# A graph-attention layer: the scaling of gathered rows takes its factors through a DVE operation that reads the newest logit

## Chip, cores, metric

One core of one Trainium2 chip. The metric is the device time of the whole program in microseconds (us). Every run below was in the fast state. Engines: PE is TensorE's matrix multiply and PEld its weight load, DVE is VectorE, ACT ScalarE, POOL GpSimd, SP SyncE.

## The reference, cut to what matters

4096 nodes with 512 features, 8 heads of 64, float32. A row of `adj` has some 17 ones; attention runs over these alone.

```python
hs = layer_norm(h_source); ht = layer_norm(h_target)
q = (ht @ Wq + bq) / sqrt(64); k = hs @ Wk + bk; v = hs @ Wv + bv
logits = where(adj != 0, q @ k^T per head, -1e30)
ctx = softmax(logits) @ v
ht = ht + ctx @ Wo + bo                  # h_target is normalized here, too
ht = layer_norm(ht)
out = layer_norm(x + ht + gelu(ht @ W1) @ W2)
```

## The kernel before

Phases that overlap: projecting all K/V rows to DRAM (`kvd`), turning the adjacency rows into lists of neighbours, and attention with the feed-forward layer. The 4096 targets are sorted by degree and handled in 32 tiles of 128. A tile is worked in supergroups of up to S neighbours (211 supergroups in all): for each, POOL gathers K/V rows, DVE multiplies K by q and reduces to logits `lg`, ACT takes the exponential, DVE multiplies V by it, and PE sums over neighbours by transposing into one PSUM tile, `cps`.

Before a tile's attention its `front` makes q. It is a generator, advanced one step (`yield`) at a time by the supergroups of earlier tiles. The first part below is where the change acts. A scheduler orders the instructions of each engine and may draw one forward past others when it expects its inputs to be there, so the position of a `yield` does not fix the place in an engine's queue. A data dependence does.

```python
def front(i, idle=0):
    rec = recs[i]                                  # the tile's record: targets, neighbours, mean and rstd
    tq = sp.tile([P, 2 * D], F32, name="tq", bufs=3)
    t = tq[:, :D]
    gather(t, h_target, rec[:, TGT:TGT + 1])       # POOL: indirect DMA of 128 rows
    for _ in range(1 + idle):
        yield
    m = rec[:, RST:RST + 2].bitcast(F32)
    nc.scalar.activation(t, t, AF.Identity, bias=m[:, 1:2], scale=m[:, 0:1])    # ACT, line 990
    yield
    pt = ps.tile([P, KC, P], F32, name="t", bufs=2)
    for kc in range(KC):
        nc.tensor.transpose(pt[:, kc, :], t[:, kc * P:(kc + 1) * P], ident)     # PE, line 994
    hT = tq[:, D:].rearrange("p (c t) -> p c t", c=KC)
    for kc in range(KC):
        nc.scalar.activation(hT[:, kc, :], pt[:, kc, :], AF.Identity, ...)      # ACT, line 997
    yield
    yield
    # ... q projection: matmuls with wq on PE, line 1003, three yields
    nc.vector.scalar_tensor_tensor(tq[:, :D], pq, HD ** -0.5, bqr, ...)         # DVE, line 1008
    tqs[i] = tq

def prefetch(i):
    # ...
    rec = sp.tile([P, E0 + MAXE], I32, name="rec", bufs=7)
    nc.gpsimd.dma_start(rec[:, :RW], recs_d[part][r0:r0 + P, :])                # record load
    recs[i] = rec

# attention, one supergroup k of tile i
nc.vector.tensor_tensor(kv[:, :n, :D], kv[:, :n, :D], tq..., ALU.mult)          # DVE, line 1209
lg = sp.tile([P, S, H], F32, name="lg")
nc.vector.tensor_reduce(lg[:, :n, :], kv..., AX.X, ALU.add)                     # DVE, line 1213
if j0 > 0:
    nc.scalar.activation(p[:, j0:j0 + n, :], lg[:, :n, :], AF.Exp)              # ACT, line 1217
advance()                                          # steps of fronts and of finished tiles' tails
# ...  the value products (line 1173) and transposes into cps (line 1181) of the supergroup before
```

Of the kernel before, what the change touches and what calls it, by code (L numbers as in the profile page):

```python
# [12 lines left out]
ALU = mybir.AluOpType  # L13
# [430 lines left out]
def adj_resnorm_kernel(  # L444
# [33 lines left out]
    nc = tc.nc  # L478
# [51 lines left out]
    def rows(a, g):  # L530
        return a[g * GR:(g + 1) * GR, :].rearrange("(j p) d -> p j d", p=P)

    with tc.tile_pool(name="keep", bufs=1) as keep:
# [17 lines left out]
        with ExitStack() as late:  # L551
# [26 lines left out]
            def xrows(n):  # L578
                return ring[:, 12 + n % 5, :].rearrange("p (j d) -> p j d", j=G)
# [183 lines left out]
            def keep_rest():  # L763

                while held:
                    nc.sync.dma_start(*held.pop())
# [97 lines left out]
            def project(order, t=None):  # L864


                state, scales = {}, {}

                def request(n, t=None):
                    if n >= len(order):  # L870
                        return
                    if t is None:
                        t = xrows(n)
                        nc.sync.dma_start(t, rows(x, order[n]))
                    state[n] = t

                def measure(n):
                    if n >= len(order):
                        return
                    mv = ip.tile([P, G, 2], F32, name="mv")  # L880
                    for j in range(G):
                        stats(ip, state[n][:, j, :], mv[:, j, :], "n1")
                    scales[n] = rstd_of(ip, mv, G, "n1")

                def scale(n):
                    if n >= len(order):
                        return
                    t, (rs, nm) = state[n], scales.pop(n)
                    for j in range(G):
                        nc.scalar.activation(t[:, j, :], t[:, j, :], AF.Identity,  # L890
                                             bias=nm[:, j:j + 1], scale=rs[:, j:j + 1])

                def turn(n):
                    if n >= len(order):
                        return
                    t = state[n]
                    hT = sp.tile([P, KC, GR], F32, name="h2T")
                    for k2 in range(KC // 2):
                        pt = (psi if k2 else ps).tile([P, 2, GR], F32, name="pt" if k2 else "t",
                                                      bufs=1 if k2 else 2)  # L900
                        for k in range(2):
                            kc = k2 * 2 + k
                            for j in range(G):
                                nc.tensor.transpose(pt[:, k, j * P:(j + 1) * P],
                                                    t[:, j, kc * P:(kc + 1) * P], ident)
                        for k in range(2):
                            kc = k2 * 2 + k
                            if n == 0:

                                nc.vector.tensor_scalar(hT[:, kc, :], pt[:, k, :],  # L910
                                                        s1c[:, kc:kc + 1], b1c[:, kc:kc + 1],
                                                        op0=ALU.mult, op1=ALU.add)
                            else:
                                nc.scalar.activation(hT[:, kc, :], pt[:, k, :], AF.Identity,
                                                     bias=b1c[:, kc:kc + 1],
                                                     scale=s1c[:, kc:kc + 1])
                    state[n] = t, hT

                def source(n, j):
                    g, hT = order[n], state[n][1]  # L920
                    if asked or moms:
                        kvr = sp.tile([P, 2 * D], F32, name="tq", bufs=3)
                    else:

                        kvr = ring[:, 8 + (n * G + j) % 3, :]
                    for half, w in enumerate((wk, wv)):
                        pkv = psi.tile([P, D], F32, name="pq", bufs=3)
                        for kc in range(KC):
                            nc.tensor.matmul(pkv, hT[:, kc, j * P:(j + 1) * P], w[:, kc, :],  # L929
                                             start=kc == 0, stop=kc == KC - 1)  # L930
                        nc.scalar.copy(kvr[:, half * D:(half + 1) * D], pkv)  # L931
                    r0 = 1 + (g * G + j) * P
                    nc.scalar.dma_start(kvd[r0:r0 + P, :], kvr)
                    return 7.8

                with tc.manual_schedule(engines={mybir.EngineType.DVE}):
                    request(0, t)
                    measure(0)
                    scale(0)
                    turn(0)  # L940
                    request(1)
                    measure(1)
                    scale(1)
                for n in range(2, 4):
                    request(n)
                measure(2)
                yield 0.0
                for n in range(len(order)):
                    for j in range(G):
                        cost = source(n, j)  # L950
                        if j == 0:
                            request(n + 4)
                            measure(n + 3)
                            turn(n + 1)
                        else:
                            scale(n + 2)
                            del state[n]
                        yield cost


            recs, tqs, h2Ts, done, ready = {}, {}, {}, set(), []

            def gather(dst, table, idx):
                nc.gpsimd.indirect_dma_start(  # L964
# [15 lines left out]
            def front(i, idle=0):  # L980


                rec = recs[i]
                tq = sp.tile([P, 2 * D], F32, name="tq", bufs=3)
                t = tq[:, :D]
                gather(t, h_target, rec[:, TGT:TGT + 1])
                for _ in range(1 + idle):
                    yield
                m = rec[:, RST:RST + 2].bitcast(F32)
                nc.scalar.activation(t, t, AF.Identity, bias=m[:, 1:2], scale=m[:, 0:1])  # L990
                yield
                pt = ps.tile([P, KC, P], F32, name="t", bufs=2)
                for kc in range(KC):
                    nc.tensor.transpose(pt[:, kc, :], t[:, kc * P:(kc + 1) * P], ident)
                hT = tq[:, D:].rearrange("p (c t) -> p c t", c=KC)
                for kc in range(KC):
                    nc.scalar.activation(hT[:, kc, :], pt[:, kc, :], AF.Identity,  # L997
                                         bias=b1r[:, kc:kc + 1], scale=s1c[:, kc:kc + 1])
                yield
                yield  # L1000
                pq = ps.tile([P, D], F32, name="t", bufs=2)
                for kc in range(KC):
                    nc.tensor.matmul(pq, hT[:, kc, :], wq[:, kc, :], start=kc == 0,  # L1003
                                     stop=kc == KC - 1)
# [3 lines that stand above are left out]
                nc.vector.scalar_tensor_tensor(tq[:, :D], pq, HD ** -0.5, bqr,  # L1008
                                               op0=ALU.mult, op1=ALU.add)
                tqs[i] = tq  # L1010
# [5 lines left out]
            kvs, rests, fronts = {}, {}, {}  # L1016
# [10 lines left out]
            def step(gens, i):  # L1027

                if i in gens and next(gens[i], StopIteration) is StopIteration:
                    del gens[i]  # L1030
# [115 lines left out]
            def first_fronts():  # L1146

                for i in range(EARLY):
                    prefetch(i)
                for i in range(EARLY):  # L1150
                    fronts[i] = front(i)
                while fronts:
                    go_on()
                    yield 4.0

            def attention():
# [41 lines left out]
                for group in GROUPS:  # L1198
# [3 lines left out]
                    for i in group:  # L1202
                        cps = ps.tile([P, KC, P], F32, name="cps", bufs=2)
                        while k < len(SG) and SG[k][0] == i:
                            _, j0, n = SG[k]
                            while i not in tqs:
# [3 lines left out]
                                                    tq[:, :D].unsqueeze(1).to_broadcast([P, n, D]),  # L1210
                                                    ALU.mult)
                            lg = sp.tile([P, S, H], F32, name="lg")
                            nc.vector.tensor_reduce(lg[:, :n, :],  # L1213
                                                    kv[:, :n, :D].rearrange("p j (h d) -> p j h d", h=H),
                                                    AX.X, ALU.add)
# [218 lines left out]
            def other_lists():  # L1434
                for cost in ed:
                    yield 1.5 * cost
                yield from sort(1)

            _weave((att, 0), (chain(feed(g) for g in range(len(GROUPS))), 0), (other_lists(), WAIT),
# [36 lines left out]
```

## Time and profile before

| | before |
|---|---|
| time, median of 3 (range) | 1851.66 us (1851.42 to 1855.57) |
| profiled span | 1847.4 us |
| PE busy | 1693.9 us, 92% |
| DVE busy | 1428.8 us, 77% |
| ACT busy | 1222.2 us, 66% |
| POOL busy | 971.7 us, 53% |

The prediction shows the busy rows and the waits of the line that the change touches. From the list of waits, these five lines matter for the rivals (who waited, for what: us in total, times, longest):

```profile
POOL kv L964 <- PE cps L1181: 157.2, 79, 17.0
...
DVE kv L1209 <- DMA kv<-kvd,rec: 71.2, 27, 11.7
ACT p L1217 <- DVE lg L1213: 69.3, 37, 9.3
ACT gt L1319 <- PE pf L1316: 66.7, 17, 8.0
...
DVE tq L1008 <- PE t L1003: 42.6, 10, 9.8
```

POOL waits for PE to free K/V slots; DVE waits for K/V rows, and for PE's projection of q before it can evict it; ACT waits for logits and for the feed-forward matmuls. A long row does no harm in itself: it tells who was idle, not whether the end moved.

One hole in PE's row as the timeline shows it (start, busy us, engine, line, operation, shapes; in brackets the wait in us and what ended it):

```profile
1294.69 3.62 PE L1316 MATMUL pf<-h2T,w 128*128 128x256 f32 x16
...
1302.12 3.70 PE L1003 MATMUL t<-wq,tq 128*128 128x512 f32 x8 [3.81 <-ACT tq L997]
```

PE finished what stood ahead, and then stood 3.81 us for ACT's eviction at line 997, which follows a blocked scaling in ACT's queue. Holes of this sort are what the change is after.

### The profile page before, as it was taken

The numbers are of one execution on the slowest core, as the hardware profiler recorded it, in microseconds if no ns is written. First come the engines' busy times: TensorE is split into PE (matmuls) and PEld (weight loads), VectorE is DVE, ScalarE is ACT, GpSimd is POOL, SyncE is SP. The second block draws the span as 40 slices with busy tenths as digits, with TensorE's granted clock in tenths as the row PEclk, the third lists the DMA queues.
The fourth block names the chain that finished last, engine by engine and source line by source line (L and its number), as shares of the span: only waits on it lengthen the run. The fifth ranks groups of instructions, "written<-read, shape, count | busy, mean of one in ns | idle before, by whom it ended". The sixth has DMA issues, their size and how long they took to land. (4 is left out here: it accounts for less than half of the span.)

```text
span 1847.4 us, 22879 instructions
## 1 busy us (share of the span) xinstructions
PE 1693.9 (92%) x7030; PEld 1101.0 (60%) x7030; DVE 1428.8 (77%) x2596; ACT 1222.2 (66%) x3121; POOL 971.7 (53%) x834
## 2 busy tenths in 40 slices
PE   7999884697988989999998998999999999999997
PEld 3444332475655656767676656666666666666664
DVE  6999855999989838686968989979787797988200
ACT  5777634587877646686767867687767676787311
POOL 1000153856546577656567787776574665664001
PEclk9999987898999989999999999999999999999999
DMA  9999949988876738677769878687676767775000
GB/s 350 374 388 374 348 156 350 348 300 303 285 271 209 243 96 313 230 252 260 275 225 315 293 265 295 221 298 253 233 265 216 251 225 247 236 248 170 12 12 25
DMA packets 144396, 463.27 MB, mean 251 GB/s; under 512 B 20628, under 2 KB 25800, under 8 KB 144264
## 3 DMA queue, kind: packets, MB, share of 16 engines
q0 software_dynamic: 96656, 342.64, 54.2%
q1 hardware_dynamic: 39792, 96.00, 14.5%
q10 hardware_dynamic: 7816, 23.08, 3.3%
q8 instruction: 58, 0.95, 0.2%
q14 instruction: 74, 0.61, 0.1%
HBM read 430.76 MB, written 30.89 MB: 250 GB/s over the span
## 5 line engine op out<-in xcount | busy, mean ns | idle before, releaser
L964 POOL DMA_INDIRECT kv<-kvd,rec x603 | 744.9, 1235 | 395.1 <-PE cps L1181 157.2
L1325 PE MATMUL po<-w,gt 128*128 128x512 f32 x1024 | 470.4, 603 | 9.7 <-ACT gt L1319 7.2
L1316 PE MATMUL pf<-h2T,w 128*128 128x256 f32 (+1 forms) x2176 | 466.6, 368 | 1.1 <-issue 0.7
L1316 PEld LDWEIGHTS pf<-h2T,w 128*128 128x128 f32 x2176 | 388.7, 191 | 66.6 <-issue 22.4
L1209 DVE TENSOR_TENSOR kv<-kv,tq 128x1536 f32<-128x1536 f32 (+2 forms) x211 | 352.0, 1676 | 82.4 <-DMA kv<-kvd,rec 71.2
L1193 ACT ACTIVATE kv<-kv,pa 128x64 f32<-128x64 f32 x1520 | 390.8, 336 | 4.1
L1213 DVE TENSOR_REDUCE lg<-kv 128x24 f32<-128x1536 f32 (+2 forms) x211 | 350.2, 1667 | 1.1 <-DVE kv L1209 0.2
L1325 PEld LDWEIGHTS po<-w,gt 128*128 128x128 f32 x1024 | 190.7, 194 | 210.3 <-issue 201.5
L1181 PE MATMUL cps<-ident,kv 128*128 128x128 f32 x2008 | 264.6, 280 | 51.1 <-DMA kv<-kvd,rec 24.2
L1181 PEld LDWEIGHTS cps<-ident,kv 128*128 128x128 f32 x2008 | 238.2, 145 | 120.2 <-DVE kv L1173 51.5
L1173 DVE TENSOR_TENSOR kv<-kv,p 128x1024 f32<-128x1024 f32 (+1 forms) x211 | 251.5, 1194 | 41.2 <-ACT p L1217 28.8
L687 POOL TENSOR_TENSOR n_rs<-n_ve,mhalf 128x2 f32<-128x2 f32 (+2 forms) x51 | 47.7, 936 | 340.8 <-DVE n_ve L680 139.8
L728 ACT ACTIVATE kv<-kv 128x1024 uint8<-128x1024 int32 x128 | 134.7, 1054 | 76.8 <-DMA kv<-in_adj_dram 40.6
L1319 ACT ACT_TABLE_LOAD x104 | 133.4, 1283 | 1.6
L735 DVE MAX8 cand<-kv 128x8 uint16<-128x103 uint16 (+1 forms) x640 | 130.2, 252 | 1.7 <-issue 0.7
L1003 PE MATMUL t<-wq,tq 128*128 128x512 f32 x256 | 119.9, 611 | 12.1 <-ACT tq L997 12.1
L1319 ACT ACTIVATE gt<-pf 128x512 f32<-128x512 f32 x128 | 76.4, 597 | 81.0 <-PE pf L1316 66.7
L929 PE MATMUL pq<-wk,h2T 128*128 128x512 f32 x256 | 121.6, 618 | 5.2 <-ACT tq L931 3.7
L929 PE MATMUL pq<-wv,h2T 128*128 128x512 f32 x256 | 118.5, 606 | 6.7 <-ACT kv L931 5.5
L1107 PE MATMUL t<-wo,rb 128*128 128x512 f32 x256 | 120.7, 614 | 0.0
L990 ACT ACTIVATE tq<-tq,rec 128x512 f32<-128x512 f32 x32 | 26.0, 813 | 142.8 <-DMA tq<-in_L_gnn_h_target_dram,rec 136.3
L1217 ACT ACTIVATE p<-lg 128x24 f32<-128x24 f32 (+2 forms) x179 | 38.9, 218 | 94.6 <-DVE lg L1213 69.3
(156 smaller groups left out, 1603.3 us busy)
## 6 DMA issues: line engine op xcount, KB each, us to landing
kv<-in_adj_dram SPq DMA_DIRECT2D x128, 512.0 KB
kvd<-tq ACTq DMA_DIRECT2D x24, 512.0 KB
kv<-kvd,rec POOLq DMA_INDIRECT x603
kv<-in_L_gnn_h_target_dram SPq DMA_DIRECT2D x32, 256.0 KB
kv<-in_x_dram SPq DMA_DIRECT2D x15, 512.0 KB
rest_d<-gid SPq DMA_DIRECT2D x32, 160.0 KB
w<-in_L_gnn_W_dram SPq DMA_DIRECT2D x4, 1024.0 KB
kvd<-kv ACTq DMA_DIRECT2D x8, 512.0 KB
```

The costliest lines, as they stand in the source:

```text
L728: nc.scalar.activation(sg, a, AF.Sign, accum_out=dpart[:, i, h:h + 1])
L735: nc.vector.max(cand[:, h * SQ + s, :], wd[:, w0:w1])
L929: nc.tensor.matmul(pkv, hT[:, kc, j * P:(j + 1) * P], w[:, kc, :], start=kc == 0, stop=kc == KC - 1)
L964: nc.gpsimd.indirect_dma_start(out=dst, out_offset=None, in_=table[:, :], in_offset=bass.IndirectOffsetOnAxis(ap=idx, axis=0))
L1173: nc.vector.tensor_tensor(v4, v4, p[:, j0:j0 + m, :].unsqueeze(3) .to_broadcast([P, m, H, HD]), ALU.mult)
L1181: nc.tensor.matmul(cps[:, c, :], kv[:, j, D + c * P:D + (c + 1) * P], ident, is_transpose=True, start=j0 + j == 0 and c == 0, stop=j0 + n ...
L1193: nc.scalar.mul(v, v, pa[:, hd:hd + 1])
L1209: nc.vector.tensor_tensor(kv[:, :n, :D], kv[:, :n, :D], tq[:, :D].unsqueeze(1).to_broadcast([P, n, D]), ALU.mult)
L1213: nc.vector.tensor_reduce(lg[:, :n, :], kv[:, :n, :D].rearrange("p j (h d) -> p j h d", h=H), AX.X, ALU.add)
L1316: nc.tensor.matmul(pf[:, k, :], w1[(f0 + k) // KC][:, kc, (f0 + k) % KC * P:((f0 + k) % KC + 1) * P], h2T[:, kc, :w], start=kc == 0, stop= ...
L1319: nc.scalar.activation(gt, pf, AF.Gelu_apprx_tanh)
L1325: nc.tensor.matmul(po[j], gt[:, k, j * P:(j + 1) * P], w2[(f0 + k) // KC][:, (f0 + k) % KC, :], start=False, stop=f0 + k == FC - 1, skip_g ...
```

## The change

Its intent: in the schedule before, the scaling of a tile's row is placed so early that ACT reaches it while the row gather is still under way. ACT then stands, and what is queued behind stands with it (at 1299.68 us it started the scaling after 4.25 us of waiting, and only then, at 1300.40, the copy behind it). The change makes the scaling depend on something that comes later by itself: a DVE operation that writes the two factors `m` back unchanged (`max(m, m)`; the bypassed operand is the newest logit). It also stores the last list's spare candidates at the end of the list phase, and makes the first two tiles, which have no logits yet, use a late K/V projection.

```diff
@@ source(): K/V projection @@
                         nc.scalar.copy(kvr[:, half * D:(half + 1) * D], pkv)
+                    if n >= 14:
+                        latest[:] = [kvr[:, 0:1]]
@@ front() @@
                 m = rec[:, RST:RST + 2].bitcast(F32)
+                nc.vector.scalar_tensor_tensor(m, m, latest[-1], m, op0=ALU.bypass, op1=ALU.max)
                 nc.scalar.activation(t, t, AF.Identity, bias=m[:, 1:2], scale=m[:, 0:1])
@@ first_fronts() @@
                     fronts[i] = front(i)
+                    step(fronts, i)
+                while not latest:
+                    yield None
@@ attention() @@
                             lg = sp.tile([P, S, H], F32, name="lg")
+                            latest[:] = [lg[:, 0, 0:1]]
@@ other_lists() @@
                     yield 1.5 * cost
+                keep_rest()
                 yield from sort(1)
```

(The list `latest` is also created; blank lines are cut.) From here on "the tie" is the added DVE operation. The lines of the changed kernel stand some lines lower: 990 is 995 there, 994 is 999, 997 is 1002, 1003 is 1008, 1008 is 1013, 1173 is 1181, 1181 is 1189, 1209 is 1217, 1213 is 1222, 1217 is 1226, 1138 is 1143, 1316 is 1325, 1319 is 1328. The tie itself is line 994 there.

More of the change, by code (lines that the diff above doesn't have):

```diff
@@ L958, in project @@
                         yield cost
-            recs, tqs, h2Ts, done, ready = {}, {}, {}, set(), []
+            recs, tqs, h2Ts, done, ready, latest = {}, {}, {}, set(), [], []
             def gather(dst, table, idx):
```

## The prediction

> **What bounds the kernel now.** I read the page first (busy shares and slices), then the table of groups by line, then the waits, then one line's own view, then the busy time in stretches of 50 us, and last the timelines around the longest stalls.
>
> ```profile
> PE 1693.9 (92%) x7030; PEld 1101.0 (60%) x7030; DVE 1428.8 (77%) x2596; ACT 1222.2 (66%) x3121; POOL 971.7 (53%) x834
> PE   7999884697988989999998998999999999999997
> DVE  6999855999989838686968989979787797988200
> ACT  5777634587877646686767867687767676787311
> ```
>
> TensorE is the fullest engine, and in the last slices it is the only one with work: attention ends near 1700 us and TensorE then works alone for 137 us on the feed-forward layer. Its work is fixed, so the span is that work plus the holes in TensorE's row. Busy shares hide some holes, so I also measured the spacing of matmul starts against the usual spacing of each form (109 ns for a 128x128 transpose, 215 for 256 columns, 429 for 512). That gives 1634 us of work and 193 us of excess spacing; the rest of the span is its two ends. Of the excess some 62 us lie before 300 us (projections and the switch to attention), 67 us between 300 and 600 us, and 64 us after. The stretches show how unevenly it lies:
>
> ```profile
> 300.00:350.00 50.00, 20.50 (x104) 16.10 (x104) 39.06 (x45) 22.53 (x82) 39.42 (x33) 0.66 1.00 386
> ...
> 700.00:750.00 50.00, 50.00 (x237) 35.32 (x236) 44.50 (x45) 38.91 (x116) 34.73 (x31) 1.00 0.84 289
> ...
> 1100.00:1150.00 50.00, 45.16 (x206) 31.35 (x204) 44.20 (x44) 35.14 (x97) 39.72 (x31) 1.00 0.91 318
> ```
>
> (Columns: window, length, then busy us and count of PE, PEld, DVE, ACT, POOL, then clock, DMA share, GB/s.) From 700 us on TensorE is nearly full; no other engine is.
>
> The instruction that the change touches is the scaling of the gathered h rows on ScalarE, line 990:
>
> ```profile
> L990 ACT ACTIVATE tq<-tq,rec 128x512 f32<-128x512 f32 x32 | 26.0, 813 | 142.8 <-DMA tq<-in_L_gnn_h_target_dram,rec 136.3 <-issue 6.5
> ...
> ACT tq L990 <- DMA tq<-in_L_gnn_h_target_dram,rec: 136.3, 28, 14.0
> ...
> PEld t L994: 7.9, 2
> PE t L994: 7.2, 2
> ```
>
> It works 26.0 us and holds ScalarE idle for 142.8 us, 28 waits of up to 14.0 us for the row gather to land. The last two lines are from the line's own view, "who waited for it": its direct consumer on TensorE lost only 7.2 us, in two places. So the 143 us harm only through whatever stands behind the blocked instruction in ScalarE's queue.
>
> **What the Trainium skill says.** (1) "Trainium Kernel Development and Optimization", Performance Expectations, warns that matmul busy time is a bad measure because matmuls are pipelined. The trace agrees: the 92% row holds 1634 us of work in 1847 (88%). (2) "Perfetto Trace Analysis", Per-instruction lifecycle (DVE / Act), puts the semaphore wait before the reported start. Agrees: the 813 ns contain no wait, the 142.8 us stand as idle time before it. (3) "DMA: Bandwidth & Descriptors", Anatomy of one DMA, fits 2.0 us plus bytes/436e3 per DMA, an estimate of 2.6 us for these 256 KB. The trace is slower: in the cases where ScalarE was already waiting, issue to use took about 3.4 to 7.7 us (590.0 to 593.6, 513.3 to 521.0). (4) "VectorE: DVE Perf Modes", the errata on SBUF sources, charges a fixed cost per instruction. Agrees: a scalar_tensor_tensor on 128x2 takes 163 ns here (line 692), though it handles two columns.
>
> **The change, part by part.** First, 32 added DVE instructions, `m = max(m, m)` on 128x2, which read the newest logit (for the first two tiles, the newest projection) without using it. Cost: 32 x 163 ns = 5.2 us of DVE, on an engine that is 77% busy; I charge 1 us to the path. Second, what moves. The order of instructions shows that the scheduler, which had drawn line 990 forward, must now place it behind that logit. Counting softmax exponentials ahead of it on ScalarE, it stands later in 27 of 32 tiles, by 1 to 9 supergroups (mostly 2 to 5); tiles 0, 1, 3, 8 and 20 do not move. TensorE's order of the transposes and projections that follow is practically the same against the context matmuls, and so is DVE's `tq` evacuation, and POOL's gathers but for two. This is then a change of ScalarE's queue alone. In the attention part a supergroup takes about 6.6 us (1395 us over 211), so two to five are 13 to 33 us, more than nearly all of the waits. What remains are tiles 0, 8 and 20, with 6.5, 5.9 and 6.9 us, and remnants where the move is one place: I expect ScalarE's wait at this line to fall from 143 to about 20 us.
>
> What is that worth? I followed each wait forward along ScalarE's queue: everything behind it could come earlier by the wait, less every later idle gap of ScalarE, which would absorb it. Wherever a TensorE stall ended by such a ScalarE instruction, I took the smaller of the stall and the surviving shift: 1.4 and 7.1 us (525 to 534), 0.9 (436), 2.0 (897), 3.6 (1089), 1.8 (1151), 1.7 (1244), 3.8 (1302), 2.0 (1388), 1.4 (1664): sum 25.7 us. The longest of them I checked in the timeline:
>
> ```profile
> 521.00 0.81 ACT L990 ACTIVATE tq<-tq,rec 128x512 f32<-128x512 f32 x1 [6.72 <-DMA tq<-in_L_gnn_h_target_dram,rec]
> ...
> 523.83 0.60 ACT L1319 ACTIVATE gt<-pf 128x512 f32<-128x512 f32 x1
> ...
> 533.06 1.92 ACT L1138 ACTIVATE h2T<-t,cols 128x256 f32<-128x256 f32 x4
> ...
> 534.12 1.11 PE L1090 MATMUL t<-ident,rb 128*128 128x128 f32 x4 [7.10 <-ACT h2T L1138]
> ```
>
> Between the block and the late eviction stands a gelu whose matmuls ended only at 522.4, so the eviction could come some 1.4 us earlier, not 6.7. That takes 5.7 us off: 20 us direct. The same walk finds up to 59 us of DVE waits that would shrink; DVE is not the bound, so I choose 5 us of them to come through to TensorE as less waiting for the value products (line 1173). Sum: 20 + 5 - 1 = 24 us.
>
> Third, new waits. The DVE instruction needs the tile's record in SBUF, which only the gathers needed before, and DVE's queue blocks behind it. For tiles 8 and 20 the record load was issued at most 5.4 and 6.6 us before the gather, beside logits that follow closely; I charge 2 us together. Fourth, the store of the last candidates (`keep_rest`): the last store was already issued at 603.5 us, the first gather that reads it at 863 us, and the queue's order is unchanged. Worth 0. The start-up line in the first two tiles: ScalarE's block at 266 to 273 us turns into a block on DVE's instruction behind a list step that ended at 274.4; the last store of K/V comes after sign activations that wait for adjacency loads in both versions. Worth 0 to 1 us; I take 0.
>
> Total 22 us: 1851.7 - 22 = **1830 us**.
>
> **Rivals.**
> A: the wait was hidden anyway. For it: the direct consumer lost 7.2 us; TensorE is in order and its order doesn't change; between 300 and 600 us its stalls are mostly start-up, where DVE has the work. Around 953 us the longest sort of block (10.1 us) lies beside a DVE gap of 9.4 us that comes from late K/V gathers, and would stay. Against it: seven stalls are ended by line 997 or 1193 or an eviction directly behind a block. It would give 1840 to 1852.
> B: the gain multiplies. Attention is a ring: ScalarE's exponential, DVE's product, TensorE's transposes, freed slots, POOL's gathers (157.2 us idle for TensorE's line 1181), then DVE again. If ScalarE's blocks pace that ring, most of the 115 us of excess after 300 us could go, and I would see 1790 to 1812. Against it: TensorE has no excess between 700 and 800 us (0.1 us), with a block of 14.0 us at 760 in it.
> C: a wait takes the removed one's place. Scaling now comes two to three supergroups before the evacuated `tq` is needed on DVE (before: mostly four to eight), and the chain of transposes, four evictions and eight passes of 0.43 us each or more must fit. DVE already waited 42.6 us for that `tq`, 9.8 us at most. Lateness there, or DVE standing for a record or scatter, would give 1845 to 1870. Against it: TensorE's order put the transposes mostly 15 to 40 us after the old scaling, usually more than the move.
>
> **Range and chances.** The middle is the mechanism at its counted size. Between A and a mild B lies 1812 to 1850, which I hold 8 times in 10. Two per cent is 37 us, below 1814.6: it needs B, 0.13. Slower than 1888.7 would need C everywhere, 0.02. Within 2%: 0.85.
>
> **What would show it.** Right: ScalarE's idle time before the scaling 10 to 30 us; TensorE's work by spacing the same and its excess after 300 us near 93 instead of 115 us; stalls at 1089, 1244, 1302 and 1388 gone; DVE's 32 new instructions near 0.16 us each with under 10 us idle before them. Wrong: the idle time gone and the excess unchanged (A), the K/V gathers' wait for TensorE's transposes down by half (B), or DVE's wait before `tq` well above 43 us (C).

## The result, and the profile after

A ratio here is the mean time of one kernel's fast runs over that of the other's in the same rounds, so it is not quite the ratio of the medians quoted beside it. Intervals are 95%.

| | before | after |
|---|---|---|
| time, median | 1853.62 us (4 runs) | 1828.03 us (4 runs: 1816.57 to 1828.37) |
| ratio | | 0.9847 (0.9806 to 0.9888), "same" by the 2% rule |
| profiled span | 1847.4 | 1826.4 |
| granted clock | 0.964 | 0.963 |
| PE work by spacing of matmul starts | 1633.9 | 1633.5 |
| PE excess spacing | 193.3 | 173.4 |

By the ratio that is 28 us (0.0153 of 1853.62), by the medians 25.6, by the two profiled executions 21.0. PE's work did not change and its excess fell by 19.9 us, so the gain of the profiled pair lies nearly all in PE's holes. The page's row:

```profile
PE 1687.8 (92%) x7030; PEld 1102.5 (60%) x7030; DVE 1432.2 (78%) x2628; ACT 1222.0 (67%) x3119; POOL 973.8 (53%) x834
ACT  5767634487987637676767777778777676787311
```

The shares hardly differ: a gain of 1.5% can't be read from them. DVE has 32 instructions more and 3.4 us more work. The own view of the scaling says what happened (first row: count, shortest/median/longest ns, first and last start; then what ended ACT's idle time before it, and below the cut who waited for it):

```profile
L995 ACT ACTIVATE tq<-tq,rec x32: 798/806/852, 278.1 to 1633.4; 128x512 f32<-128x512 f32 x32
...
  DMA tq<-in_L_gnn_h_target_dram,rec: 15.3, 2
  DVE rec L994: 13.5, 4
  issue: 2.1, 2
...
  PE t L999: 15.4, 5
```

142.8 us of idle time became 30.9. Two waits for a gather are left (tile 8 with 6.3 us and tile 20 with 9.0), and four for the tie, of which 11.3 us is the first tile's. PE's transposes now lose 15.4 us here, 7.2 before; 7.4 us of it is the first tile's. The tie's own view:

```profile
L994 DVE SCALAR_TENSOR_TENSOR rec<-rec,lg x30: 171/215/267, 341.3 to 1631.4; 128x2 f32<-128x2 f32 x30
...
  DMA rec<-rec: 4.7, 2
```

Its median is 215 ns. The 32 durations sum to 6.9 us, of which DVE's busy row shows 3.4. DVE stood 4.7 us in two places for a record that had not landed. Of the waits:

```profile
POOL kv L966 <- PE cps L1189: 161.4, 89, 8.7
ACT p L1226 <- DVE lg L1222: 114.1, 52, 11.0
ACT gt L1328 <- PE pf L1325: 87.8, 20, 9.6
DVE kv L1217 <- DMA kv<-kvd,rec: 82.9, 22, 12.3
...
DVE tq L1013 <- PE t L1008: 46.5, 14, 8.3
```

Part of ACT's freed time turns up as other waits. The rows of ACT waiting for logits and for feed-forward matmuls grew by 44.8 and 21.1 us, 66 of the 112 us that went from the scaling's row. Such rows are no measure of the gain: the start-only kernel below, which kept the gather waits and gained nothing, has 100.1 and 72.2 us in them. ACT's busy time is the same (1222.2 and 1222.0).

The same three stretches of 50 us as in the prediction:

```profile
300.00:350.00 50.00, 20.01 (x80) 15.93 (x81) 37.64 (x41) 22.47 (x79) 38.86 (x32) 0.56 0.99 385
...
700.00:750.00 50.00, 50.00 (x227) 34.14 (x226) 37.38 (x47) 39.62 (x106) 32.55 (x29) 1.00 0.82 282
...
1100.00:1150.00 50.00, 45.88 (x209) 33.04 (x210) 49.27 (x51) 40.90 (x110) 41.43 (x29) 0.97 0.83 293
```

The first two gained nothing. In the third PE has a little more work done, and DVE 5 us more. Summed over stretches of 100 us, PE's excess spacing fell most from 500 to 600 us (20.4 to 9.8), from 1200 to 1300 (8.0 to 1.8), from 400 to 500 (18.5 to 14.1), from 1300 to 1400 (4.1 to 0.1) and from 1100 to 1200 (10.3 to 6.7), and rose from 300 to 400 (28.0 to 31.9), from 1000 to 1100 (9.5 to 12.8) and from 800 to 900 (3.9 to 6.6). The stretches are of each kernel's own time, so a stall that moved over an edge counts as a fall and a rise.

The two timelines, first the stall at 534 us that the prediction showed:

```profile
526.70 0.60 ACT L1328 ACTIVATE gt<-pf 128x512 f32<-128x512 f32 x1
527.19 1.92 ACT L1143 ACTIVATE h2T<-t,cols 128x256 f32<-128x256 f32 x4
...
529.45 0.85 ACT L995 ACTIVATE tq<-tq,rec 128x512 f32<-128x512 f32 x1
...
528.26 0.66 PE L1095 MATMUL t<-ident,rb 128*128 128x128 f32 x4 [2.74 <-ACT h2T L1143]
```

Before, ACT did the scaling at 521.0, with 6.72 us of waiting, then two gelus, at 523.83 and 532.33, and 0.73 us after the start of the second the eviction of `h2T` at 533.06. Now the two gelus are at 514.70 and 526.70, the eviction is 0.49 us behind the second, and the scaling comes after both, without a wait. PE's stall went from 7.10 to 2.74 us.

The other place is the hole at 1302 us. PE's order is the same there, and the matmul that waited (the 4790th of PE's 7030) now starts at 1287:

```profile
1283.79 3.62 PE L1325 MATMUL pf<-h2T,w 128*128 128x256 f32 x16
1287.25 3.60 PE L1008 MATMUL t<-wq,tq 128*128 128x512 f32 x8
```

PE runs from one group into the next without a hole.

### The profile page after: what moved, and what is told of

It is laid out like the page before. It is cut to its first block, busy times and chain, and to the rows that moved or that the text cites. A ratio compares the mean times of both kernels' runs of the same rounds, so it can differ in the third digit from the quotient of the medians.

```text
span 1826.4 us, 22937 instructions
## 1 busy us (share of the span) xinstructions
PE 1687.8 (92%) x7030; PEld 1102.5 (60%) x7030; DVE 1432.2 (78%) x2628; ACT 1222.0 (67%) x3119; POOL 973.8 (53%) x834
## 5 line engine op out<-in xcount | busy, mean ns | idle before, releaser
L966 POOL DMA_INDIRECT kv<-kvd,rec x603 | 751.4, 1246 | 376.2 <-PE cps L1189 161.4
L1334 PE MATMUL po<-w,gt 128*128 128x512 f32 x1024 | 464.9, 597 | 6.2 <-ACT gt L1328 6.0
L1217 DVE TENSOR_TENSOR kv<-kv,tq 128x1536 f32<-128x1536 f32 (+2 forms) x211 | 351.7, 1675 | 88.1 <-DMA kv<-kvd,rec 82.9
L1189 PE MATMUL cps<-ident,kv 128*128 128x128 f32 x2008 | 269.0, 283 | 53.4 <-issue 23.5
L1189 PEld LDWEIGHTS cps<-ident,kv 128*128 128x128 f32 x2008 | 243.3, 147 | 122.4 <-issue 68.9
L1181 DVE TENSOR_TENSOR kv<-kv,p 128x1024 f32<-128x1024 f32 (+1 forms) x211 | 250.9, 1193 | 23.8 <-ACT p L1226 20.3
L1328 ACT ACTIVATE gt<-pf 128x512 f32<-128x512 f32 x128 | 76.3, 597 | 99.2 <-PE pf L1325 87.8
L1226 ACT ACTIVATE p<-lg 128x24 f32<-128x24 f32 (+2 forms) x179 | 39.2, 219 | 128.8 <-DVE lg L1222 114.1
L1112 PE MATMUL t<-wo,rb 128*128 128x512 f32 x256 | 116.5, 597 | 0.0
L929 PEld LDWEIGHTS pq<-wk,h2T 128*128 128x128 f32 x256 | 50.3, 203 | 72.9 <-issue 59.1
```

The lines of the kernel that those rows point to most:

```text
L929: nc.tensor.matmul(pkv, hT[:, kc, j * P:(j + 1) * P], w[:, kc, :], start=kc == 0, stop=kc == KC - 1)
L966: nc.gpsimd.indirect_dma_start(out=dst, out_offset=None, in_=table[:, :], in_offset=bass.IndirectOffsetOnAxis(ap=idx, axis=0))
L1181: nc.vector.tensor_tensor(v4, v4, p[:, j0:j0 + m, :].unsqueeze(3) .to_broadcast([P, m, H, HD]), ALU.mult)
L1189: nc.tensor.matmul(cps[:, c, :], kv[:, j, D + c * P:D + (c + 1) * P], ident, is_transpose=True, start=j0 + j == 0 and c == 0, stop=j0 + n ...
L1217: nc.vector.tensor_tensor(kv[:, :n, :D], kv[:, :n, :D], tq[:, :D].unsqueeze(1).to_broadcast([P, n, D]), ALU.mult)
L1328: nc.scalar.activation(gt, pf, AF.Gelu_apprx_tanh)
```

## The experiments

Theory: ACT's queue, blocked by the gather in front of ready work, delayed evictions that PE needed; the tie moves the scaling behind them. Rivals for the source of the gain: the start-up lines or the store of the candidates; a nonlinear effect on the ring of K/V slots; the later place of the tile's transposes on PE rather than the wait. Rivals for what limits it: DVE's added work, or DVE's waits for q and for records. The edits below are against the changed kernel unless they say otherwise. The kernel before ran on the same chip in each call (medians 1856.79, 1854.42, 1854.88 and 1857.33 us in the four calls).

A kernel that has only the added store was built but not run: its order of instructions on all five engines is that of the kernel before (the author's comparison; no trace of it is kept).

### The tie without the store

```diff
 def other_lists():
-                keep_rest()
```

> The change without its second part (the earlier store of the last candidates). The order of instructions on every engine is the same as in the changed kernel, so my theory expects 1828 us, within 3 us. A rival that gives the store a share of the 25 us would expect 1835 us or more.

Measured: 1825.65 us (6 runs, 1818.73 to 1838.51), ratio 0.9831 (0.9797 to 0.9866). Its order of instructions on every engine is that of the changed kernel. The whole gain is here, so the store is worth nothing that can be seen.

### The tie in the first half, and in the second half

```diff
+                if i < 16:            # the other kernel: if i >= 16
                     nc.vector.scalar_tensor_tensor(m, m, latest[-1], m, ...)
```

> Only tiles 0 to 15 take their factors through the DVE operation; the other 16 scalings stand on ScalarE where they stood before. By spacing of matmul starts the changed kernel lost 10 us less than the kernel before up to 900 us and 12 us less after. My theory (each freed wait pays where it stands) expects 1843 us, 1838 to 1847. A rival that puts the gain into the start of attention or into one place expects nearly all of it here (1830) or nothing (1852).

> The other half: only tiles 16 to 31 are tied. My theory expects 1841 us, 1836 to 1846, and the gains of both halves to add up to that of the whole, within 5 us. The rival of one early place expects 1852 us.

Measured: 1844.61 us, ratio 0.9939 (0.9906 to 0.9972), and 1841.41 us, ratio 0.9923 (0.9886 to 0.9961). The waits of the scaling that are left, first with the tie up to tile 15, then with the tie from 16:

```profile
ACT tq L996 <- DMA tq<-in_L_gnn_h_target_dram,rec: 82.7, 16, 9.9
```

```profile
ACT tq L996 <- DMA tq<-in_L_gnn_h_target_dram,rec: 64.4, 12, 13.9
```

Each half loses the waits of its own tiles and keeps the others'. The gains, 0.61 and 0.77%, sum to 1.38% (25.6 us of 1856.79), beside 1.69% for the whole in the same call; the intervals of the halves are about 0.35% wide to each side, so the sum and the whole agree. That fits a sum of local gains, spread over the whole attention part. It is no sign of a ring that speeds up only when all waits are gone.

### The wait put back, everything else kept

A copy of one column onto itself, on ACT, ahead of the tie: it needs the gathered row and nothing else, so the scheduler may place it as early as it did the scaling before.

```diff
+                nc.scalar.copy(t[:, 0:1], t[:, 0:1])
                 nc.vector.scalar_tensor_tensor(m, m, latest[-1], m, ...)
                 nc.scalar.activation(t, t, AF.Identity, bias=m[:, 1:2], scale=m[:, 0:1])
```

> The changed kernel with one 128x1 copy of a gathered column onto itself on ScalarE, which the scheduler puts where the scaling stood before (the same place among the exponentials in 31 of 32 tiles). It brings back ScalarE's wait for the row gather and nothing else; the scaling stays late. My theory (it is the blocked queue that costs) expects ScalarE to idle 110 to 150 us before these copies and the time to return to 1846 to 1858 us. The rival (the order of the scaling itself, or the later transposes, makes the gain; the waits were hidden) expects 1828 to 1835 us.

Measured: 1847.93 us (1842.54 to 1854.79), ratio 0.9965 (0.9929 to 1.0001). In the order of ACT's queue the copy stands where the scaling stood before in 31 of 32 tiles. With the copies left out, the order of instructions on DVE and POOL is that of the changed kernel throughout, and on PE and ACT but for five neighbours that changed places; the real scaling has the same number of exponentials ahead of it in all 32 tiles. So this kernel is the changed kernel plus the old wait. The copy's own view, and one row of the waits (from line 994 on, this kernel's lines stand one lower again than the changed kernel's):

```profile
L994 ACT COPY tq<-tq x32: 191/191/194, 275.7 to 1645.0; 128x1 f32<-128x1 f32 x32
...
  DMA tq<-in_L_gnn_h_target_dram,rec: 136.4, 27
...
ACT p L1227 <- DVE lg L1223: 76.9, 43, 9.3
```

The stall at 534 us again, in this kernel:

```profile
523.84 0.19 ACT L994 COPY tq<-tq 128x1 f32<-128x1 f32 x1 [8.56 <-DMA tq<-in_L_gnn_h_target_dram,rec]
...
534.38 0.60 ACT L1329 ACTIVATE gt<-pf 128x512 f32<-128x512 f32 x1
534.87 1.93 ACT L1144 ACTIVATE h2T<-t,cols 128x256 f32<-128x256 f32 x4
...
535.94 1.11 PE L1096 MATMUL t<-ident,rb 128*128 128x128 f32 x4 [6.70 <-ACT h2T L1144]
```

ACT's order around it is the changed kernel's, and the stall is back: 7.10 us before, 2.74 in the changed kernel, 6.70 here. So is the hole at 1302 us (3.81, none, 3.23).

The wait is back (136.3 us before, 136.4 here), ACT's wait for logits fell back from 114.1 to 76.9 (before: 69.3) and that for feed-forward matmuls from 87.8 to 62.7 (before: 66.7), and PE's excess is 194.0 (before 193.3, after 173.4). Of the 31.4 us that the tie gave in this call (0.0169 of 1856.79), 24.9 are gone and 6.5 are left (0.0035), with an interval that touches no gain. The tie and the later places of the real scaling are all still there. So the removed wait on ACT is the cause of at least most of the gain. The remaining 6.5 us, if real, may come from the 0.8 us of the scaling itself, which no longer stands right behind each wait (the copy takes 0.19); that was not tested. The start-up lines are not the source (the start alone, below, gives 1.0009).

### The scaling one supergroup later still

```diff
-                for _ in range(1 + idle):
+                for _ in range(1 + idle + 2 * (i >= EARLY)):
```

> The changed kernel with every scaling from tile 2 on one supergroup (about 6.6 us) later still, the projection's deadline on DVE unchanged. If the room behind the scaling is used up, DVE's wait before the evacuated tq (46.5 us in the changed kernel) rises above 70 us and TensorE waits for the scaling in many tiles: 1835 to 1870 us. The rival, that later is always better or at least free, expects 1820 to 1830 us.

Measured: 1828.94 us (1826.45 to 1830.82), ratio 0.9858 (0.9835 to 0.9882): no loss, so the expectation failed. The wait that should have grown did:

```profile
DVE tq L1013 <- PE t L1008: 72.9, 17, 10.4
```

46.5 us became 72.9 and the time did not change. DVE's waits for K/V rows went from 82.9 to 47.9 us in the same run: perhaps DVE reaches the next K/V tile later and finds it there. Where one such row grows as another shrinks, neither by itself tells what the end waits for. PE's transposes moved later along with the scaling here, and that did not help either.

### The start alone

```diff
+                if i < EARLY:
                     nc.vector.scalar_tensor_tensor(m, m, latest[-1], m, ...)
```

> Only tiles 0 and 1 (the start of attention) take their factors through the DVE operation; the hand-over of the first fronts is as in the changed kernel. My theory gave this part 0 to 1 us: 1848 to 1857 us, same as before within half a per cent. It also tells whether the missing 6 us of the run with the early read come from the hand-over: then this run is 5 us or more faster than before.

Measured: 1854.47 us (14 runs), ratio 1.0009 (0.9988 to 1.0031). The start-up lines are worth nothing.

### The front one step earlier, with the tie and without

```diff
-                for _ in range(1 + idle):
+                for _ in range(max(1, idle - 1)):
```

> The changed kernel with the scaling one supergroup earlier in 22 tiles, still tied to the logit. It takes back about half of the move. My theory expects part of ScalarE's waits for the gather to return (50 to 90 us against 15) and the time to lie between: 1830 to 1845 us. A rival by which the tie itself, not its distance, makes the gain expects 1825 to 1830 us.

Measured: 1878.26 us, ratio 1.0134 (1.0109 to 1.0159), far off what was expected. The edit was a poor one: besides the scaling it moved PE's transposes and projections of 28 tiles one supergroup earlier, and DVE's evictions of q in some. To tell the tie's part from the shift's, the same edit was made in the kernel before, without any tie:

> The run with the scaling one supergroup earlier was 2.7 per cent slower than the changed kernel, not between it and before as I expected. Its order shows that it moved more than the scaling: TensorE's transposes and projections of 28 tiles also stand one supergroup earlier, and some row gathers later. This run makes the same shift in the kernel before, without the tie. If TensorE's earlier order is what costs (it then waits for a front that is not ready), this run is slower than before by 20 to 50 us, 1875 to 1905, and the tie's gain is still inside the earlier run. If the shift only hurts together with the tie, it is at 1850 to 1858 us.

Measured: 1880.26 us, ratio 1.0139 (1.0109 to 1.017). The shift alone costs about 25 us, which explains the miss. From the waits of this kernel:

```profile
DVE kv L1209 <- DMA kv<-kvd,rec: 130.3, 41, 12.6
```

DVE's waits for K/V rows are 130.3 us here and 128.1 with the tie, where they were 71.2 and 82.9 without the shift; PE's excess is 224.1 and 220.5. But with the shift the tie gives next to nothing (1.0134 beside 1.0139), though it takes the scaling's idle time from 117.1 to 48.2 us. It may be that DVE, waiting for K/V rows, sets the pace there, and that ACT's blocks are then hidden behind it. Which of its consequences makes the shift so costly was not taken apart and stays open.

### The tie four times, beside the changed kernel again

```diff
-                nc.vector.scalar_tensor_tensor(m, m, latest[-1], m, ...)
+                for _ in range(4):
+                    nc.vector.scalar_tensor_tensor(m, m, latest[-1], m, ...)
```

> The changed kernel with the DVE operation four times in a row, 96 instructions of 0.2 us more, 20 us of DVE, each waiting for the one before it. I charged the 32 operations with 1 us on the path. If that is right for the size of the operation, this run is at 1828 to 1834 us; if DVE is on the path with them, 1840 to 1850 us.

> The changed kernel once more, unaltered, for a ratio from this chip beside the two others and for the spread of its runs (one of the four runs of the first measurement was at 1816.6 us): 1820 to 1832 us, ratio 0.980 to 0.989. The store alone cannot differ, so it should agree with the run without the store (0.9831).

Measured: four times 1835.14 us (1827.42 to 1840.96), ratio 0.9883 (0.9849 to 0.9916); the changed kernel unaltered 1831.62 us (1830.37 to 1834.67), ratio 0.9875 (0.9846 to 0.9904). 96 more operations, some 20 us by their own durations (DVE's busy row grew by 12.6, from 1432.6 to 1445.2), cost 1.5 us by the ratios and 3.5 by the medians, within the intervals. So the tie's own 32 operations cost about 1 us (0.5 to 1.2 by these figures, up to some 3 by the intervals), and DVE's work is not what limits the gain.

### Record loads on another queue

An attempt at a faster version: the record loads of later tiles by SP's queue, so that POOL need not stand for a freed record buffer ahead of its gathers.

```diff
-                nc.gpsimd.dma_start(rec[:, :RW], recs_d[part][r0:r0 + P, :])
+                (nc.sync if i >= 12 else nc.gpsimd).dma_start(rec[:, :RW], recs_d[part][r0:r0 + P, :])
```

> The changed kernel with the records of tiles 12 to 31 loaded from the SyncE queue, so that POOL's queue no longer stands behind the scatter of an earlier tile (28.3 us in 15 waits in the changed kernel). For tile 20 the gather and the scaling should come earlier and TensorE's 3.3 us stall at 1198 us shrink. My estimate: POOL's waits for the scatter down to some 8 us, time 1818 to 1827 us. If those waits are hidden behind TensorE, 1826 to 1831 us.

Measured: 1835.19 us, ratio 0.99 (0.9874 to 0.9925); no gain. POOL's wait for the output rows to be stored moved from the record load (24.5 us in the changed kernel) to the next indirect DMA (24.5 us), and 11.3 us stayed on the record loads that POOL kept: the wait followed POOL's queue and was not removed (28.3 us in all became 35.8). The last matmul came at 1811.6 us (changed kernel: 1813.4), and still the span was 1832.9. The difference is POOL's closing operation, and the one before it (2.38 us in place of 0.66). The second kernel keeps the last tiles' loads on POOL (`12 <= i < 28`), to see whether their place at the end matters:

> As the run with the records of tiles 12 to 31 on the SyncE queue, but the last four tiles' records stay on POOL. That run lost at the end: its last matmul was at 1811.6 us, 2 us before the changed kernel's, but POOL's closing drain took 8.97 us instead of 1.95, and the instruction before it 2.38 instead of 0.66. It also did not remove POOL's waits for the scatters (35.8 us), it moved them to the next gather. If the drain depends on plain loads that POOL issues late, it is back at 1.95 us here and the time at 1822 to 1831 us; if it depends on how many POOL issues in all, it stays at 6 us or more and the time at 1830 to 1838 us. I do not expect a gain over the changed kernel beyond its noise.

Measured: 1836.76 us (1826.92 to 1848.15), ratio 0.9892 (0.9845 to 0.9939). The closing operation in the changed kernel, with 20 loads moved, and with 16 moved (shortest/median/longest ns of three):

```profile
L1481 POOLq DRAIN  x3: 44/107/1952, 1823.6 to 1826.1; - x3
```

```profile
L1481 POOLq DRAIN  x3: 44/107/8975, 1823.1 to 1832.6; - x3
```

```profile
L1481 POOLq DRAIN  x3: 44/107/9302, 1826.3 to 1836.2; - x3
```

1.95 us became 8.97 and 9.30. In all twelve traces that kept the loads on POOL it is 1.95. So late loads on POOL's queue do not bring the short closing back. Why it grows was not settled; these traces tell only that it goes with having moved the loads. No version here is faster than the changed kernel.

## Why the prediction was right

Predicted were 1830 us and a range of 1812 to 1850; measured were 1828.03 us. Step by step:

- **The bound.** TensorE's work plus its holes: right. Work by spacing 1633.9 and 1633.5 us, excess down by 19.9 of the 21.0 us between the two spans. The prediction's "near 93 instead of 115 us" after 300 us counted only stalls above 150 ns, which it did not say: by that count 115.7 fell to 90.5, and came back to 112.0 with the wait put back. All excess after 300 us fell from 131.6 to 110.
- **The wait at the scaling.** About 20 us were expected, 10 to 30; it was 30.9. Tiles 8 and 20 kept theirs as named (5.9 and 6.9 us expected, 6.3 and 9.0 measured). Tile 0 was worse, 11.3 us in place of 6.5, now a wait for the tie. The start-only kernel shows that this costs nothing at the end.
- **What the wait is worth.** 143 us of blocked queue, 20 us direct: right in total, and the kernel with the wait put back shows that the wait is the cause. PE's stalls above 150 ns after 300 us that ended with an ACT instruction fell from 63.2 to 43.2 us (40.3 and 39.4 in the two other traces with this order of instructions, the changed kernel again and the tie without the store). Not every stall went as listed. The stalls at 1147, 1302, 1388 and 1664 us are gone; the one at 1242 shrank only from 1.86 to 1.52. The 3.8 us at 1089 are gone, but close by PE loses 5.2 us at 1098 (1.7 before) and 1.5 at 1092, to DVE. At 897 it grew, from 2.1 to 3.5 us. At 534 the gain was 4.4 in place of 1.4 us, because the working misread a gelu. Two stand between the block and the eviction, and each follows one group of 16 matmuls, in order. Those matmuls that ended at 522.4 feed the second, at 532.33; the gelu at 523.83, which the prediction shows, belongs to the group that ended at 513.75. Neither held the eviction to 1.4 us. So the 5.7 us should not have been taken off, and that 20 still fits is partly luck: this error and the others cancel.
- **DVE's 5 us.** This did not come true. The waits of the value products fell from 41.2 to 23.8 us (all releasers, from the groups by line), but PE did not wait less for them: its stalls that they ended were 22.4 us before and 25.2 after, and all that DVE ended rose from 25.5 to 34.1 (37.4 and 40.8 in those two traces; same count as above). The total held because stalls with no releaser named fell from 27.1 to 13.1 us (17.5 and 20.0), which was not forecast. That is luck, too.
- **DVE's added work.** 5.2 us at 163 ns were expected, 1 us charged. The operation took 215 ns, 6.9 us in all, and the kernel with four of each shows about 1 us at the end.
- **Records.** 2 us charged; DVE stood 4.7 us for them in two places. The run one supergroup later shows none of this wait and is no faster, but it moved other things, too, so the cost at the end stays open.
- **Store and start, 0.** Right by two runs (0.9831 without the store; 1.0009 with the start alone) and by the identical order of instructions.
- **Rivals.** A, hidden anyway, was right of most of the wait: 112 us less of it made 21 to 31 us. It was wrong of the rest, as the kernel with the wait put back shows. B, a ring that multiplies, falls: POOL's wait for PE's transposes was 157.2 and is 161.4, and the two halves add up. C: DVE's wait before q rose only from 42.6 to 46.5, and the later version shows that even 72.9 costs nothing.

## What to carry to other kernels

A long wait of an in-order engine is worth only what the instructions queued behind it were needed for: follow each one to the stall that it ends. Most of the wait can be hidden: here 112 us of it gave 21 to 31, and in the kernel with the front one step earlier 69 us of it gave nothing. Where a scheduler draws an instruction forward to a place where its input is late, a small true dependence on something later in the program puts it back, at the price of one short operation. To show that the wait, and not the new place, is the cause, put the wait back by itself: a one-column read of the same data at the old place was enough.

## What the Trainium skill lacked or had wrong

- "VectorE: DVE Perf Modes", the section on the errata: the table's fixed cost of 58 cycles would make an operation on two columns 60/0.96 = 62.5 ns (an estimate from that table). The section's own formula for a float32 `tensor_tensor` add, (N+151)/0.96, gives 159 (an estimate, too), near line 692's 163. The tie, which also reads a per-partition scalar, took 171 to 267 ns, with a median of 215; neither form covers it.
- No page says what makes POOL's closing drain longer. It was 1.95 us in the changed kernel (and in every other trace that kept its loads on POOL) and 8.97 and 9.30 us where 20 and 16 of its 32 record loads had gone to SP's queue, more than the 1.8 us by which the last matmul of the former came earlier.
- No page says how to value the wait of one instruction for what is queued behind it. Here 112 of 142.8 us were removed, worth 21 to 31 us of the span, and putting 136.4 us back cost about 25.
